# Four steps of a selective-scan layer moved one slot later in a hand-written schedule

## The chip, the cores and the metric

The kernel runs on one core of one Trainium2 chip. The metric is the device time of one execution in microseconds (us). All data are float32.

The engines have short names in the profile. PE is the matrix engine, and PEld is its weight load, which overlaps it. DVE is the vector engine, ACT the scalar engine, POOL the GpSimd engine, and SP the engine that issues most of the transfers. SBUF is the on-chip memory, and PSUM the small memory that PE writes its products to.

## The reference

The input x has the shape (2, 128, 64, 64): two images of 128 channels with 64 x 64 = 4096 positions. Four operators follow each other:

1. an embedding (a 128 x 128 product), two layers of a state-space model with a feed-forward net, an output product and a residual;
2. self-attention over the 4096 positions, whose query, key and value come from 3 x 3 convolutions;
3. self-attention whose query, key and value come from 1 x 1 products;
4. a multi-scale block: convolutions at four scales, a small attention over the scales, a layer norm and a fusion.

The change touches the two layers of operator 1 alone. One of these layers computes, for the tokens t of an image:

```
r = t;  x = layernorm(t)
u, z = split(x @ in_w.T);  u = silu(causal_conv4(u) + conv_b)
dt, B, C = split(u @ xproj_w.T);  dt = softplus(dt @ dt_w.T + dt_b)
h[n] = exp(dt * A[n]) * h[n] + dt * u * B[n]      # along the positions, 16 states n, 256 channels
y = sum_n h[n] * C[n] + u * ssm_D                 # the skip term
y = y * silu(z)                                   # the gate
t = y @ out_w.T + r                               # the mixer's output and its residual
t = t + ffn_w2 @ gelu(ffn_w1 @ layernorm(t))      # with biases
```

## The kernel before

**Items and slots.** The layers work on items. An item is a chunk of 512 positions of one image in one layer, so there are 2 images x 2 layers x 8 chunks = 32 items, in this order. For each item the scan is done in 32 steps of 128 rows x 512 positions: 8 groups (`g`, 32 channels each, four states side by side on the partitions make 128 rows) with 4 steps each. Each step is a *slot*. The outer loop (`for i in range(-2, NI + 2)`) runs over items, the inner one over the 32 slots. A period is one turn of the outer loop.

**What a slot always issues,** in this order: at the first slot of a group the transfers of dt for a later group (`spread_dt`), the product that spreads dt*u for the next group into the one PSUM buffer `pdu` (`spread_dtu`, L334, PE), and every second group the product that sums h over the states into `py` (`y_pair`, L373, PE, for two groups at once); then the scan of this slot (L358, DVE); the decay of four slots later (L347, ACT, four PSUM buffers `da`, so it waits for the scan of its own slot); after the last slot of a group, on POOL, a copy of the carries (L360) and the product of h with C (L361); and on DVE `times_b` (L340), which makes h for the next group from B and `pdu`. The h buffers are a ring of five that also holds `hid`, the feed-forward net's hidden values; a new h thus waits until the product `py` of an old one has been computed.

**The background steps.** All other work of the layers is spread over the slots by `background(i)`: `at(t, f, ...)` puts a step into slot t of period i. Steps go out behind the scan, the decay and `times_b` of their slot. Each engine takes its instructions in the order in which they are issued; no scheduler reorders them. In period i the scan belongs to item i, n = i + 1 is prepared (convolution and projections), p = i - 1 is finished (second half of y, gate, mixer, second layer norm), q = i - 2 ends its feed-forward net, and r = i + 2 is embedded and normalised. An item has an embedding (`embed`, L187; `embed_out`, L191) if r is in the first layer, and an output product (`out_mm`, L429; `out_add`, L434) if q is in the second.

**The steps that the change names.**
- `y_out` (L381, DVE): u = u * D + py, for one half (128 channels) of an item. It reads `py` in PSUM. Half 0 of item i is due in its own period, half 1 in the next.
- `gate` (L384, POOL): z = z * u over both halves.
- `mix_out` (L390 and L391, PE): the mixer's product into the PSUM buffer `po`, with the residual added through an identity.
- `mix_add` (L394, ACT): copies `po` back into the image.

**What is issued near them.** On DVE the scans and `times_b`. On PE, behind `py` in slot 4, the last convolution taps (L262), a z projection (L275), the feed-forward net's second product (L415 and L417), `pdu`, and then `mix_out`. On ACT a long row starts at `mix_add`: the silu with two table loads (L282 and L283, slot 11), `embed_out` or `out_add`, the squares and centred values of the layer norms (L203 and L204, from `pc`, L196), `dbl` (L295, from `pd`, L291), and the softplus with its table loads (L315 and L316, slot 17), with decays between them. The softplus frees `dtu` (L321, POOL, slot 18) and `var` (L210, PE); behind `var` come `ve` (L214, ACT) and further decays, behind `dtu` come h of that group and `nt` (L226, POOL), and then `nt` on ACT (L227, slot 20) and decays again. `ln_scale` (L239, DVE) waits for `pr` (L235, PE) in slot 28.

The loop that issues a slot:

```
if 0 <= t < NT:
    scan(t)
if 0 <= t + 4 < NT:
    decay(t + 4)
if m == 3 and 0 <= g + 1 < NG:
    times_b(g + 1)
for f, a in todo[t_]:
    f(*a)
```

Of the kernel before, what the change touches and what calls it, by code (L numbers as in the profile page):

```python
# [67 lines left out]
def tile_conv_seq(ctx: ExitStack, tc, x, consts, vecs, wemb, wlay, wconv, wdt, wqkv, wsmall, wms, out):  # L68
# [39 lines left out]
    with ExitStack() as s, tc.manual_schedule():  # L108
# [25 lines left out]
        for l in range(NL):  # L134
# [15 lines left out]
            for g in range(4):  # L150
                pa = mm.tile([P, NJ, DS], F32, name="pa", tag="mm")
                nc.tensor.matmul(pa.rearrange("p j n -> p (j n)"), lhsT=four(g), rhs=an, start=True, stop=True)
                for q in range(4):
                    at = slice(32 * q, 32 * q + 32)
# [15 lines left out]
        def has(i):  # L170
            return 0 <= i < NI
# [265 lines left out]
        def background(i):  # L437

            todo = [[] for _ in range(NSL)]

            def at(t, f, *a):
                todo[t].append((f, a))

            n, p, q, r = i + 1, i - 1, i - 2, i + 2
            if has(q):
                at(3, gelu, q)
                at(6, ffn_down, q, (0, 1)), at(7, ffn_down, q, (2, 3)), at(9, ffn_add, q)
                at(11, out_mm, q), at(12, out_add, q)
            if has(p):
                at(6, y_out, p, 1), at(6, gate, p)  # L450
                at(8, mix_out, p), at(10, mix_add, p)
            if has(n):
                at(0, pu_taps, n, 0, (0, 1)), at(1, pu_taps, n, 0, (2, 3)), at(2, pu_out, n, 0)
                at(3, pu_taps, n, 1, (0, 1)), at(4, pu_taps, n, 1, (2, 3)), at(5, pu_out, n, 1)
                at(13, xproj, n), at(14, xproj_out, n), at(14, spread_bc, n)
                at(15, dtproj, n, 0), at(16, dtproj, n, 1), at(17, soft_plus, n), at(18, dt_end, n)
            if has(i):
                at(1, pz_mm, i, 0), at(3, pz_out, i, 0)
                at(5, pz_mm, i, 1), at(6, pz_out, i, 1)
            if has(i) or has(n):  # L460
                at(11, silu, i, n)
            pair = [(k, second) for k, second in ((p, True), (r, False)) if has(k)]
            if has(r):
                at(10, embed, r), at(11, embed_out, r)
            w, m = {}, len(pair)
            for k, (it, second) in enumerate(pair):
                at(12 + 2 * k, ln_centre, w, k, it)
                at(13 + 2 * k, ln_square, w, k, it)
                at(27, ln_spread, w, k, m), at(28, ln_scale, w, k, it)
                at(29, ln_shift, w, k, it, second)  # L470
            if pair:
                at(17, ln_var, w, m), at(18, ln_eps, w, m), at(19, ln_rs, w, m), at(20, ln_newton, w, m), at(21, ln_step, w, m)
            if has(p):
                for f in range(4):
                    at(30 + f // 2, ffn_up, p, f)
            if has(i):
                at(23, y_out, i, 0)
            return todo

        eps = wp.tile([P, 1], F32, name="eps")  # L480
# [4 lines left out]
        for i in range(-2, NI + 2):  # L485
            todo = background(i)
            for t_ in range(NSL):
                t = i * NSL + t_
                g, m = divmod(t, 4)
                if m == 0 and 0 <= g + 3 < NG:  # L490
                    spread_dt(g + 3)
                if m == 0 and 0 <= g + 1 < NG:
                    spread_dtu(g + 1)
                if m == 0 and g % 2 == 1 and 0 <= g - 3 < NG:
                    y_pair(g - 3)
# [8 lines that stand above are left out]
# [667 lines left out]
```

## Time and profile before

| what | value |
|---|---|
| median of 3 runs | 5333.72 us (5329.3 to 5339.19) |
| span of the profiled execution | 5331.3 us |
| layers (0 to about 2190 us): PE, DVE, ACT, POOL busy | 1908, 1893, 1511, 1444 us |
| both attentions (to about 4490 us): PE, DVE busy | 2256, 1364 us |
| multi-scale block (to the end): PE, DVE busy | 745, 540 us |
| granted PE clock in these three stages | 0.88, 0.99, 0.94 |
| scans (L358) | 1024, 1265 ns each |
| `times_b` (L340) | 256, 2264 ns each |
| h times C (L361) | 256, 4532 ns each |
| skip terms (L381) | 64, 746 ns each |
| gate (L384) | 32, 2361 ns each |
| copy of `po` (L394) | 32, 588 ns each |

In a line of the timeline the first number is the start in us from the span's beginning and the second the time to the end of the group. Then follow the engine, the line of the kernel, the operation, what it writes and reads, and how many instructions were merged; in brackets stands how long the engine was idle before it and what ended that. PE's ends are modelled. A clock of 0.50 means that PE was granted half its full speed.

### The profile page before, as it was taken

Reading aid. Unit: us, or ns where it says so; the run is one execution under the profiler, and the core shown is the slowest. Engines: PE = TensorE matmul, PEld = TensorE weight load, DVE = VectorE, ACT = ScalarE, POOL = GpSimd, SP = SyncE. Lnnn points to the kernel's source line nnn. Section 1 sums busy time; section 2 is a strip of 40 time slices with the busy share of each in tenths; the row PEclk is TensorE's granted clock in tenths of the full one; section 3 lists DMA queues with packets and bytes.
Section 4 is the critical chain, followed back from the end, with each engine's and each line's share of the span. In section 5 each row is a group of like instructions: output and inputs, shape, how many; then the busy total and the mean of one; then the engine's idle time right before and its main releaser. Section 6 shows DMA issues by size and latency. Waiting matters only on the chain.

```text
span 5331.3 us, 48726 instructions
## 1 busy us (share of the span) xinstructions
PE 4908.7 (92%) x15085; PEld 2306.1 (43%) x15085; DVE 3796.5 (71%) x3810; ACT 2326.8 (44%) x2933; POOL 2286.9 (43%) x1948
## 2 busy tenths in 40 slices
PE   5899899999988997899999999999999998988997
PEld 1222222222222222356665566656666665333332
DVE  4999999999999999046663366657767775656665
ACT  4677777777777776212221122223223221223332
POOL 3766766666667667012221122223333332322221
PEclk8888988888888888999999999999999999999998
DMA  4222222222233332024442244444444442000000
GB/s 112 67 64 66 66 69 69 70 68 65 64 69 75 73 70 51 18 53 96 95 95 51 49 96 95 95 104 110 113 101 97 112 112 71 4 4 4 6 6 8
DMA packets 233843, 362.04 MB, mean 68 GB/s; under 512 B 87648, under 2 KB 88048, under 8 KB 225136
## 3 DMA queue, kind: packets, MB, share of 16 engines
q1 hardware_dynamic: 184432, 291.76, 23.3%
q10 hardware_dynamic: 49152, 67.17, 5.3%
q8 instruction: 121, 1.98, 0.2%
q14 instruction: 138, 1.13, 0.1%
HBM read 83.92 MB, written 6.29 MB: 17 GB/s over the span
## 4 chain that ended last, share of the span: by engine, by line
PE 58%; DVE 13%; POOL 12%; issue 7%; DMA 3%; ACT 3%; SPq 3%; ACTq 0%; DVEq 0%; POOLq 0%
PE pq L600 12%; PE po L647 12%; POOL h L361 9%; PE py L373 5%; PE pp L544 5%; DVE tr L627 4%; PE pu L262 3%; SPq L638 3%; PE pf L861 2%; DVE h L358 2%; DMA pt<-tr 2%; PE pdu L334 2%; PE ph L403 2%; PE pqkv L888 2%; PE pqq L544 2%
## 5 line engine op out<-in xcount | busy, mean ns | idle before, releaser
L634 POOL COPY pt<-tr 32x512 f32<-32x512 f32 x1024 | 628.0, 613 | 1680.6 <-DVE tr L627 912.0
L358 DVE TENSOR_TENSOR_SCAN h<-da,carry,h 128x512 f32<-128x512 f32 x1024 | 1241.1, 1265 | 52.0 <-ACT da L347 21.5
L361 POOL TENSOR_TENSOR h<-h,cb 128x2048 f32<-128x2048 f32 x256 | 1160.1, 4532 | 20.7 <-POOL carry L360 0.2
L604 DVE TENSOR_SCALAR_CACHE_REDUCE sc<-pq 128x1024 f32<-128x1024 f32 x512 | 625.6, 1222 | 761.0 <-PE pq L600 748.8
L647 PE MATMUL po<-pt,vt 128*128 128x256 f32 x4096 | 968.0, 380 | 4.1 <-DMA pt<-tr 4.1
L600 PE MATMUL pq<-k,q 128*128 128x512 f32 x2048 | 962.1, 592 | 4.8 <-ACT q L532 3.4
L647 PEld LDWEIGHTS po<-pt,vt 128*128 128x128 f32 x4096 | 776.4, 190 | 264.4 <-issue 174.6
L347 ACT ACTIVATE da<-dtb,am 128x512 f32<-128x512 f32 x1024 | 687.6, 685 | 273.0 <-DVE h L358 265.6
L613 ACT ACTIVATE sc<-sc,nm 128x4096 f32<-128x4096 f32 x128 | 474.8, 3710 | 723.2 <-DVE nm L611 628.0
L627 DVE STREAM_TRANSPOSE tr<-sc 128x2048 f32<-128x2048 f32 x256 | 589.2, 2302 | 37.7 <-DMA pt<-tr 24.2
L340 DVE TENSOR_TENSOR h<-bb,pdu 128x2048 f32<-128x2048 f32 x256 | 579.5, 2264 | 41.1 <-issue 28.5
L373 PE MATMUL py<-h,sel 128*32 128x512 f32 x2048 | 521.1, 654 | 0.5 <-POOL h L361 0.5
L600 PEld LDWEIGHTS pq<-k,q 128*128 128x128 f32 x2048 | 383.5, 190 | 277.8 <-issue 248.7
L334 PE MATMUL pdu<-dtu,fsel 128*128 128x512 f32 x512 | 334.4, 740 | 125.5 <-DVE h L340 123.0
L373 PEld LDWEIGHTS py<-h,sel 128*32 128x32 f32 x2048 | 117.6, 120 | 428.0 <-issue 422.4
L532 ACT ACTIVATE q<-pqq,vec 128x256 f32<-128x256 f32 x64 | 30.3, 473 | 606.4 <-PE pqq L544 361.2
L544 PE MATMUL pp<-xt,wq 128*128 128x512 f32 x576 | 250.2, 595 | 6.8 <-DMA wq<-in_wqkv 6.4
L262 PE MATMUL pu<-xn,wu 128*128 128x512 f32 x512 | 245.1, 612 | 3.3 <-ACT xn L252 1.7
L334 PEld LDWEIGHTS pdu<-dtu,fsel 128*128 128x128 f32 x512 | 97.1, 219 | 342.5 <-DVE h L340 219.6
L888 PE MATMUL pqkv<-f,ws 128*128 128x512 f32 x384 | 197.4, 640 | 10.2 <-ACT q L895 6.3
L950 DVE TENSOR_TENSOR ov<-v,pw 128x2048 f32<-128x2048 f32 x64 | 146.1, 2283 | 60.2 <-PE pw L943 60.0
L360 POOL COPY carry<-h 128x4 f32<-128x4 f32 x256 | 47.6, 186 | 317.4 <-DVE h L358 313.7
(191 smaller groups left out, 5138.1 us busy)
## 6 DMA issues: line engine op xcount, KB each, us to landing
pt<-tr SPq DMA_DIRECT2D x2048, 64.0 KB, 2.0
dtb<-dt SPq DMA_DIRECT2D x1024, 64.0 KB, 2.0
pt<-tr ACTq DMA_DIRECT2D x1024, 64.0 KB, 2.1
bb<-dr SPq DMA_DIRECT2D x128, 256.0 KB, 4.5
cb<-dr SPq DMA_DIRECT2D x128, 256.0 KB, 7.6
xt<-in_x SPq DMA_DIRECT2D x16, 256.0 KB, 5.1
xr<-in_x SPq DMA_DIRECT2D x16, 256.0 KB, 2.9
out<-ot SPq DMA_DIRECT2D x16, 256.0 KB, 2.0
```

The costliest lines, as they stand in the source:

```text
L334: nc.tensor.matmul(pdu, lhsT=four(s_ % 4), rhs=st[i]["dtu"][:, s_ // 4, :], start=True, stop=True)
L340: nc.vector.tensor_tensor(h, st[i]["bc", 0], pdu.unsqueeze(1).to_broadcast([P, 4, CH]), ALU.mult)
L347: nc.scalar.activation(da, st[i]["dtb", s_], AF.Exp, scale=am[items[i][1]][:, j, gg, m : m + 1])
L358: nc.vector.tensor_tensor_scan(h[:, m, :], da, h[:, m, :], carries[b, l][:, j, gg, m : m + 1], ALU.mult, ALU.add)
L361: nc.gpsimd.tensor_tensor(h, h, st[i]["bc", 1], ALU.mult)
L373: nc.tensor.matmul(py[r : r + 32, :], lhsT=sel, rhs=st[i]["h", s_ + k][:, m, :], start=(m == 0), stop=(m == 3), tile_position=(0, r),)
L544: nc.tensor.matmul(ps, lhsT=wq[:, which, tap, :], rhs=rhs, start=(tap == 0), stop=(tap == 8))
L600: nc.tensor.matmul(pq[:, i, :], lhsT=st["q", r, grp][:, it * P : (it + 1) * P], rhs=st["k"][:, at : at + CH], start=True, stop=True)
L604: nc.vector.tensor_scalar(dst, pq, 1.0, None, ALU.mult, ALU.max, accum_out=st["mx"][:, c2 : c2 + 1])
L627: nc.vector.transpose(tr, half.rearrange("p (t r f) -> p r t f", r=NB, f=32))
L634: nc.gpsimd.tensor_copy(dst, src)
L647: nc.tensor.matmul(st["po", r, grp], lhsT=st["vt"][:, jt, :], rhs=rhs, start=(jt == 0), stop=(jt == N // P - 1))
```

## The change

Five calls of `at` get a slot that is one later: both halves of the skip term, the gate, the mixer's product (slots 8 and 9 hold no other background product), and, from slot 10 to 11, the copy of its result. No instruction is added, removed or altered. In slot 11 the copy is still issued ahead of the silu.

```diff
             if has(p):
-                at(6, y_out, p, 1), at(6, gate, p)
-                at(8, mix_out, p), at(10, mix_add, p)
+                at(7, y_out, p, 1), at(7, gate, p)
+                at(9, mix_out, p), at(11, mix_add, p)
...
             if has(i):
-                at(23, y_out, i, 0)
+                at(24, y_out, i, 0)
```

## The prediction

> **What bounds the kernel now.** I read the engine shares and the slices of the page first, then the granted clock over one period of the layers, then the waits of line 381, then the timelines of the four engines over that period.
>
> ```profile
> PE 4908.7 (92%) x15085; PEld 2306.1 (43%) x15085; DVE 3796.5 (71%) x3810; ACT 2326.8 (44%) x2933; POOL 2286.9 (43%) x1948
> PEclk8888988888888888999999999999999999999998
> ```
>
> The edited lines run only in the first 16 to 17 slices (to about 2190 us). There PE is nearly always busy, at a granted clock of 0.88, and DVE is 86% busy (1892.88 of 2190 us). Neither share says which waits decide, so I follow one period (32 slots, one item). The 32 executions of the gate (line 384) start 64.80 to 64.90 us apart in 16 of the 31 intervals. This is one such period, cut where the clock changes; columns are busy time of PE, PEld, DVE, ACT, POOL, then clock:
>
> ```profile
> 370.56:377.38 6.82, 5.38 (x6) 0.85 (x6) 5.70 (x5) 5.70 (x8) 4.70 (x3) 0.50 1.05 229
> 377.38:384.21 6.83, 5.91 (x22) 1.79 (x22) 6.01 (x5) 5.01 (x9) 5.92 (x5) 1.00 0.72 156
> 384.21:394.45 10.24, 7.13 (x14) 1.41 (x15) 10.14 (x10) 4.49 (x7) 8.31 (x4) 0.50 0.23 57
> 394.45:435.40 40.95, 40.41 (x110) 13.47 (x106) 36.97 (x28) 31.47 (x45) 25.93 (x11) 1.00 0.10 26
> ```
>
> PE is solid for the last 41 us and runs twice at half clock. The stretches are 2, 2, 3 and 12 times 3.413 us, together 19.
>
> DVE (start, duration, what; in brackets its idle time before):
>
> ```profile
> 376.89 1.28 DVE L358 TENSOR_TENSOR_SCAN h<-da,carry,h 128x512 f32<-128x512 f32 x1 [1.02 <-ACT da L347]
> 378.09 2.26 DVE L340 TENSOR_TENSOR h<-bb,pdu 128x2048 f32<-128x2048 f32 x1
> 381.18 0.75 DVE L381 SCALAR_TENSOR_TENSOR u<-u,vec,py 128x512 f32<-128x512 f32 x1 [0.82 <-PE py L373]
> 381.84 4.80 DVE L358 TENSOR_TENSOR_SCAN h<-da,carry,h 128x512 f32<-128x512 f32 x4
> ...
> 411.62 0.75 DVE L381 SCALAR_TENSOR_TENSOR u<-u,vec,py 128x512 f32<-128x512 f32 x1 [2.16 <-PE py L373]
> ```
>
> The two skip terms make DVE wait for py, 0.82 us at slot 23 and 2.16 us at slot 6 (over the run 91.5 us in 57 waits). ACT and POOL in the same period:
>
> ```profile
> 354.67 0.68 ACT L347 ACTIVATE da<-dtb,am 128x512 f32<-128x512 f32 x1
> 357.40 0.59 ACT L394 COPY xt<-po 128x512 f32<-128x512 f32 x1 [2.06 <-PE po L391]
> 357.89 0.70 ACT L347 ACTIVATE da<-dtb,am 128x512 f32<-128x512 f32 x1
> 371.26 1.26 ACT L315 ACTIVATE dt<-pt,vec 128x512 f32<-128x512 f32 x2
> ...
> 372.60 2.34 POOL L321 TENSOR_TENSOR dtu<-dt,u 128x1024 f32<-128x1024 f32 x1 [4.85 <-ACT dt L315]
> 379.66 1.27 POOL L226 TENSOR_TENSOR nt<-nt,ve 2x512 f32<-2x512 f32 x1
> ...
> 388.88 2.08 PE L334 MATMUL pdu<-dtu,fsel 128*128 128x512 f32 x2 [3.11 <-DVE h L340]
> ```
>
> ACT waits 2.06 us for the mixer's po with a decay queued behind it, and then runs without a gap until after dt. So the loop is: PE solid from pdu (388.88) to the next po (422.21); the mixer's residual copy and 15.1 us of ACT to the end of dt; then either var on PE, ve, the last decay and scan 23 on DVE, or dtu, h and nt on POOL and decay 25 on ACT; then DVE's scans 25 to 27 and line 340, and pdu again.
>
> **What the Trainium skill says.** "TensorE: Matmul & The Clock Gate", Part 1 (What's actually happening): the clock is 4/8 or 8/8 and is judged over a free-running window of 4096 cycles at 1.2 GHz, 3413 ns. The trace agrees: only 0.50 and 1.00, changes 3.413 us apart, and a period of 19 x 3.413 = 64.85 us. The same page, Architectural detail: ACT, DVE and GpSimd queues are strict FIFO; the decay at 357.89 stuck behind the copy shows it. "GPSIMD Engine Reference", section 1: GpSimd shares its SBUF interface with VectorE where the latter has two SBUF inputs. Line 361's time here is 4503 to 4568 ns whatever DVE does, so I charge the moved gate nothing for new neighbours.
>
> **The change part by part.** Nothing is added or removed; no DMA is in the moved steps, and the order on SP and on PE stays as it was. Only DVE, ACT and POOL swap neighbours.
>
> 1. Second skip term, slot 6 to 7. DVE runs scan 7 (1.18 us, its decay was done at about 405.7) inside the 2.16 us wait. Line 340 then stands ahead of the skip term; it writes the h buffer that py reads (five buffers), so it waits for the same py and starts at about 411.65 instead of 413.48. DVE is about 1.2 us ahead at slot 8. Downstream PE is solid, and the next line 340 needs pdu at its end (about 0.3 us of the gain goes there); nothing on PE waits for DVE until pdu at slot 28. On the period: 0.
>
> 2. Gate, slot 6 to 7. It now stands behind h of that group on POOL: scan 7 ends at 410.7, carry and h to 415.5, gate to 417.9 (2.36 us). po starts at 419.50: slack 1.6 us, so 0.
>
> 3. Residual copy, slot 10 to 11 (mix_out, 8 to 9, has no PE neighbour to pass). The decay of slot 11 now runs in the 2.06 us wait ahead of the copy, so the silu and all behind it to dt come 0.62 us earlier. That holds where PE keeps ahead: in items with an embed alone pd and pc allow it; with out_mm alone pd allows 0.17; with both, PE's pc and pd bind and it is about 0. var, ve and scan 23 follow: 0.62 us.
>
> 4. First skip term, slot 23 to 24. Before: line 340 ends at 380.35, waits to 381.18, skip term, scan 24, and scan 25 starts at 383.04. After (0.62 earlier): 379.73, scan 24 to 381.0, py is ready, skip term to 381.75, scan 25. Decay 25 by the POOL path (dt, dtu, h, nt) is ready at 381.6, so it hardly binds. Gain at scan 25: 1.29 us, of which 0.67 from this step. Scans 26, 27 and line 340 carry it to pdu.
>
> Sum at the same half-clock loss: nine periods with embed alone x 1.3 = 11.7; eight with out_mm alone x 0.83 (0.17 + 0.66) = 6.6; two at the tail x 0.8 = 1.6; eight with neither x 0.7 (there 0.6 from ACT, and POOL's path limits step 4) = 5.6; four with both 0 (scan 25 there waits for decay 25 already, 0.19 us). Together 25.5 us.
>
> The clock. PE restarts at 388.88 and stays at half clock to 394.45: (394.45 - 388.88) / 2 = 2.79 us lost. The window it restarts in began at 387.63, 1.25 us earlier. If PE starts before that edge, a full window makes it warm at 391.04: an early item does so (restart at 195.50, py takes 4.79 us instead of 5.38). Short of the edge a gain is eaten: restarting earlier by d costs d/2 more, so the period stays at 19 windows until the loss reaches that of a restart at the edge, (394.45 - 387.63) / 2 = 3.41, that is for gains up to 3.41 - 2.79 = 0.62 us. Both 0.83 and 1.3 pass it. Then the restart drifts over the window, the loss lies between 1.71 and 3.41, on average 2.56, 0.23 less: 17 periods x 0.23 = 4 us more. If the out_mm periods, which pass narrowly, stay locked, it is 18 + 2 = 20 us. I take 28.
>
> The sum is against the profiled span of 5331.3 us, inside the other runs (5329.3 to 5339.2); from the median 5333.7 it gives 5306.
>
> **Rivals.** (A) Locked: the half-clock window swallows the gain and most periods stay at 64.85. For: neighbouring periods agree to 0.03 us, and items with both embed and out_mm, with 0.9 to 1.7 us more on PE, have nearly the same (64.73 to 65.12). Against: the early periods and those with neither (63.13, 63.79) do run free. Time: only the neither periods gain, 5334 - 6 = 5328. (B) Larger gain: the free periods settle on 18.5 windows (63.15, as one period does now) or the first half-clock stretch shortens as well: 27 x 1.7 = 46 us, 5288. (C) Slower: the gate now behind h is late for po. It has 1.6 us at 419.50; were scan 7 not ready to run before py, gate would end at 412.8 + 7.2 = 420.0, PE would idle 0.5 us in every item and everything behind it too, DVE's gain would be void, and 32 x 0.5 = 16 us gives 5350. It decides once gate comes over 1.6 us later than worked out. Against: decay 7 precedes the gelu on ACT and is done 5 us before. (D) Hidden: POOL's path to decay 25 binds more than I think, leaving step 3 alone: 9 x 0.62 + 8 x 0.17 + 8 x 0.6 = 11.8 us, 5322.
>
> **How the numbers follow.** Forecast 0.55, (A) 0.13, (B) 0.14, (C) 0.08, (D) 0.10. A difference of 0.2%, 10.7 us, is about what a measurement tells from none. Faster takes the forecast, (B) and (D): 0.79; same is (A): 0.13; slower is (C): 0.08. The range reaches from (B) to just past (A): 5284 to 5332. The forecast's own range is 5296 to 5318.
>
> **What would show it.** After: the waits of line 381 fall from 91.5 us to under 20; the copy at line 394 no longer has a decay between it and the silu's table load; gates come unevenly, about 63 to 64 us apart, instead of 64.85; PE's restart stretches are half-clock for 2 or 3 windows in turn; behind 2190 us all stages keep their length. Wrong if gates stay 64.85 apart with line 381's wait gone (A), or if po waits for z (C).

## The result, and the profile after

The changed kernel takes 5298.99 us (median of 4 runs, 5296.11 to 5301.44) against 5333.02 for the one before (4 runs too): the ratio is 0.9935, with a 95% interval of 0.9918 to 0.9952. It is 34 us faster; the forecast was 28 us. The two executions that were profiled differ by 37.3 us (spans of 5331.3 and 5294.0).

The engine shares and the clock row of the page after:

```profile
PE 4882.0 (92%) x15085; PEld 2303.4 (44%) x15085; DVE 3801.3 (72%) x3810; ACT 2328.5 (44%) x2933; POOL 2288.2 (43%) x1948
PEclk8899889888989898899999999999999999999998
```

The instructions are as many as before, and DVE, ACT and POOL are as busy. PE's busy time is 27 us less, with more 9s in the clock row of the layers (6 against 1 in its first 17 slices): the same products ran for less time at half clock.

The waits of DVE at line 381 (us in total, times); before it was 91.5 us in 57 waits:

```profile
  PE py L373: 8.6, 1
```

The timeline of DVE, and behind the dots those of ACT, POOL and PE, in the period that answers to the one shown of before:

```profile
376.59 1.28 DVE L358 TENSOR_TENSOR_SCAN h<-da,carry,h 128x512 f32<-128x512 f32 x1
377.79 0.72 DVE L381 SCALAR_TENSOR_TENSOR u<-u,vec,py 128x512 f32<-128x512 f32 x1
379.57 3.63 DVE L358 TENSOR_TENSOR_SCAN h<-da,carry,h 128x512 f32<-128x512 f32 x3 [1.06 <-ACT da L347]
...
408.38 2.29 DVE L340 TENSOR_TENSOR h<-bb,pdu 128x2048 f32<-128x2048 f32 x1 [1.01 <-PE py L373]
410.58 0.74 DVE L381 SCALAR_TENSOR_TENSOR u<-u,vec,py 128x512 f32<-128x512 f32 x1
...
378.24 0.72 ACT L227 ACTIVATE nt<-nt,c 2x512 f32<-2x512 f32 x1 [2.80 <-POOL nt L226]
378.87 3.88 ACT L347 ACTIVATE da<-dtb,am 128x512 f32<-128x512 f32 x6
...
416.15 1.29 ACT L347 ACTIVATE da<-dtb,am 128x512 f32<-128x512 f32 x2
419.00 0.59 ACT L394 COPY xt<-po 128x512 f32<-128x512 f32 x1 [1.56 <-PE po L391]
419.60 1.28 ACT L282 ACT_TABLE_LOAD   x1
432.26 1.27 ACT L315 ACTIVATE dt<-pt,vec 128x512 f32<-128x512 f32 x2
...
412.19 2.37 POOL L384 TENSOR_TENSOR z<-z,u 128x1024 f32<-128x1024 f32 x1
...
416.22 1.88 PE L390 MATMUL po<-z,wl 128*128 128x512 f32 x4
```

The first skip term (377.79) stands behind a scan and no longer waits. Line 340 (408.38) waits for py in place of the second one. On ACT two decays (416.15) run ahead of the copy of po, and the silu's table load follows the copy at once. The gate ends at 414.56 and po starts at 416.22, so it had 1.66 us to spare. That holds for most periods, but not for the first one, where PE waits for the gate:

```profile
160.67 3.78 PE L390 MATMUL po<-z,wl 128*128 128x512 f32 x4 [3.77 <-POOL z L384]
```

New in the period shown is the 1.06 us that scan 25 (379.57) waits for its decay, which stands behind the nt step of ACT, which waits for POOL.

The last gate starts at 2109.6 us, 35.1 us earlier than before (2144.7). What follows it takes 3184.4 us, against 3184.5 in a kernel in which only the second skip term and the gate are moved (below). So all of the gain lies in the layers.

The table gives the mean distance between two gates in us, by what the period holds, with the number of such periods in brackets. The last two periods are left out. Where the gate was moved, the first period, with an embedding, holds PE's wait for it. The distances are those of one profiled run each, which can lie some us from the median: that of the delay took 5345.7 us and was the slowest of its 13.

| kernel | us (median) | embed alone (9) | neither (8) | out_mm alone (8) | both (4) |
|---|---|---|---|---|---|
| before | 5333.0 | 64.71 | 63.99 | 64.86 | 64.88 |
| changed | 5299.0 | 63.20 | 62.44 | 63.72 | 64.86 |
| mixer's output and copy alone | 5319.1 | 63.34 | 63.10 | 64.77 | 64.91 |
| first skip term alone | 5312.8 | 63.92 | 63.17 | 63.50 | 64.61 |
| second skip term and gate alone | 5333.5 | 64.97 | 63.99 | 64.86 | 64.88 |
| before, with a delay on ACT | 5341.3 | 64.63 | 64.88 | 64.82 | 65.03 |
| changed, second skip term and gate put back | 5305.7 | 63.29 | 62.87 | 63.72 | 64.96 |
| changed, newton step later | 5280.4 | 62.49 | 62.35 | 63.16 | 63.99 |
| before, PE kept busy | 5279.6 | 62.32 | 62.38 | 62.37 | 63.87 |
| changed, PE kept busy | 5254.9 | 61.42 | 61.84 | 61.95 | 63.77 |
| changed, both | 5239.1 | 61.31 | 61.07 | 61.44 | 62.40 |

### The profile page after: what moved, and what is told of

It reads as the page before. It is cut to its first block, busy times and chain, and to the rows that moved or that the text cites. A ratio compares the mean times of both kernels' runs of the same rounds, so it can differ in the third digit from the quotient of the medians.

```text
span 5294.0 us, 48723 instructions
## 1 busy us (share of the span) xinstructions
PE 4882.0 (92%) x15085; PEld 2303.4 (44%) x15085; DVE 3801.3 (72%) x3810; ACT 2328.5 (44%) x2933; POOL 2288.2 (43%) x1948
## 4 chain that ended last, share of the span: by engine, by line
PE 47%; POOL 22%; issue 11%; DVE 10%; SPq 4%; DMA 3%; ACT 3%; ACTq 0%; DVEq 0%; POOLq 0%
POOL h L361 17%; PE pq L600 12%; PE po L647 12%; PE pp L544 5%; DVE tr L627 4%; SPq L638 3%; DMA pt<-tr 2%; PE pf L861 2%; PE pqkv L888 2%; PE pqq L544 2%; PE py L373 1%; PE pw L943 1%; POOL dtu L321 1%; POOL z L384 1%; PE pfus L1008 1%
```

## The experiments

My theory had two parts. Two moves (the copy behind a decay on ACT, and the first skip term) shorten the loop. And the loop is held at whole clock windows of 3.413 us by the half clock at which PE restarts, so that small gains and small delays are swallowed. The rivals were that gains simply add up, and that the second skip term's wait of 2.16 us was what held the loop. A period of 64.8 to 64.9 us is called held here, a shorter one free.

**One part alone.** The mixer's output and the copy:

```diff
-                at(8, mix_out, p), at(10, mix_add, p)
+                at(9, mix_out, p), at(11, mix_add, p)
```

> Only mix_out and mix_add are moved (slots 9 and 11); skip terms and gate stay. Theory (window lock): in the periods with an embedding ACT's row to dt starts 0.62 us earlier, but the period is held at 19 windows (64.85 us) for gains up to 0.62, so about nothing comes of it there; the eight periods with neither embed nor out_mm run free and gain 0.6 each: about 5328. Rival (gains simply add up): 9 x 0.62 + 8 x 0.17 + 8 x 0.6 = 12 us, 5321. Rival (the two skip terms are all that matters): 5333.

Measured: 5319.05 us, ratio 0.9967 (0.9954 to 0.9979). The periods with out_mm stay at 64.77 as expected. Those with an embedding get free, which I had put just out of reach of 0.62 us. They then gain 1.37 us, over twice what the move takes from ACT's row. Gates of three of these periods:

```profile
220.72 2.35 POOL L384 TENSOR_TENSOR z<-z,u 128x1024 f32<-128x1024 f32 x1 [4.03 <-DVE u L381]
283.28 2.36 POOL L384 TENSOR_TENSOR z<-z,u 128x1024 f32<-128x1024 f32 x1 [4.02 <-DVE u L381]
346.95 2.36 POOL L384 TENSOR_TENSOR z<-z,u 128x1024 f32<-128x1024 f32 x1 [4.02 <-DVE u L381]
```

They lie 62.56 and 63.67 us apart, together 126.23; 37 windows of 3.4133 us are 126.29. The loop has gone from 19 windows to 18.5 on average. So neither the strict lock nor the plain sum was right in size, though the total, 5319, lies near the plain sum (5321).

The periods with out_mm alone, for which 0.17 us was worked out, show the restart taking back part of a small gain. In one of them PE restarts at 1985.65 us, 4.50 us after the clock fell, and gets its full clock back at 1991.39; in the kernel before, the same restart (2003.38) comes 4.67 us after the fall, and the full clock at 2008.96. So the restart comes earlier against the clock, spends 5.74 in place of 5.58 us at half clock, and loses half of that, 2.87 in place of 2.79 us. The periods themselves are 64.85 us in both.

The first skip term:

```diff
-                at(23, y_out, i, 0)
+                at(24, y_out, i, 0)
```

> Only the first skip term is moved (slot 23 to 24). Without the earlier ACT row its gain ends where decay 25 is ready (382.2 in the shown period of before, scan 25 started at 383.04): at most 0.7 us. Window lock: 0.7 is just at the edge of what 64.85 us holds, so the periods either stay or get free by little: 5323 to 5333. Rival (gains add up): 17 x 0.67 = 11 us, 5322. The wait of line 381 at slot 23 goes; the 2.16 us at slot 6 stay.

Measured: 5312.77 us, ratio 0.9955 (0.9943 to 0.9968), and 72.2 us in 32 waits left at line 381. All but the periods with both get free. It gains more than either theory gave. Each against its own kernel before, the two parts gain 15.7 and 21.9 us, some 38 together, about as much as the whole change (34), but not in the same kinds of period.

The second skip term and the gate:

```diff
-                at(6, y_out, p, 1), at(6, gate, p)
+                at(7, y_out, p, 1), at(7, gate, p)
```

> Only the second skip term and the gate are moved (slot 6 to 7). Theory: line 340 takes over the wait for py, DVE gains 1.2 us at slot 8, PE is solid behind it and nothing comes of it: 5333, within 3 us. Rival (the 2.16 us wait was what held the loop): 27 periods x 1.2 = 32 us, 5301, that is the whole gain of the change.

Measured: 5333.5 us, ratio 0.9999 (0.9991 to 1.0007). The longer of the two waits was worth nothing by itself, and the periods with neither or with out_mm alone are unchanged to 0.01 us: the rival falls. Two effects at the ends cancel. From scan 27 of the first item to that of the third it takes 3.6 us longer (PE waits 3.77 us for the first gate, as in the changed kernel). From scan 27 of the last item but one to the end it takes 3.4 us less (3264.8 against 3268.2).

**A delay of known size.** A copy whose result nobody reads, behind the silu:

```diff
             nc.scalar.preload_act_table_set(EXP_LN_SET)
+            nc.scalar.copy(spare, kc)
```

> The kernel before with one added ACT copy of 128x656 behind the silu in slot 11 (about 0.7 us by the 128x512 and 128x1024 rows), whose result is not used: a delay of known size in ACT's row to dt. Theory (window lock): the half-clock loss at PE's restart can fall from 2.79 to 1.71 us, so the periods held at 64.85 us stay there to within 0.05 us and only the eight free periods and the ends pay: 5340. Rival (no lock): every period is 0.7 us longer, 65.5 us, and the time is 30 x 0.7 = 21 us longer, 5354.

Measured: 5341.28 us, ratio 1.0011 (1.0003 to 1.0019). The delay itself, in the timeline of ACT:

```profile
365.62 0.74 ACT L284 COPY spare<-kc 128x656 f32<-128x656 f32 x1
```

It holds ACT's row up by 0.64 us (the next instruction starts at 366.26) in every period. The held periods did not get longer (64.63 and 64.82 against 64.71 and 64.86), and the free ones went from 63.99 to 64.88: they were caught too. Three gates of periods with neither:

```profile
609.55 2.36 POOL L385 TENSOR_TENSOR z<-z,u 128x1024 f32<-128x1024 f32 x1 [2.85 <-DVE u L382]
674.25 2.36 POOL L385 TENSOR_TENSOR z<-z,u 128x1024 f32<-128x1024 f32 x1 [4.01 <-DVE u L382]
739.07 2.36 POOL L385 TENSOR_TENSOR z<-z,u 128x1024 f32<-128x1024 f32 x1 [4.02 <-DVE u L382]
```

The distances are 64.70 and 64.82 us. About 6.6 us were paid where some 20 us of delay were put in. The time is the one that the theory gave (5340), but the delay was not swallowed where the theory had it. PE's restart loses 2.77 us in the period shown, against 2.79. What gave way is the other product at half clock, var. First the kernel before, then the one with the delay, in the same period (the line numbers behind the added one are higher by 1):

```profile
372.00 3.57 PE L210 MATMUL var<-sq,kc 128*2 128x512 f32 x4 [1.54 <-ACT dt L315]
375.61 0.68 ACT L214 ACTIVATE ve<-var,eps 2x512 f32<-2x512 f32 x1 [1.08 <-PE var L210]
```

```profile
375.05 2.39 PE L210 MATMUL var<-sq,kc 128*2 128x512 f32 x4 [1.54 <-ACT dt L316]
377.51 0.66 ACT L214 ACTIVATE ve<-var,eps 2x512 f32<-2x512 f32 x1
```

With the delay the clock fell at 376.27, in the middle of var; before, it had fallen at 370.56, ahead of it. From the start of dt to that of ve it is 4.35 us before (371.26 to 375.61) and 3.20 with the delay (374.31 to 377.51). That is 1.15 us less, more than the 0.64 us put in. All eight periods with out_mm alone go the same way: var took 3.57 us in each before, and takes 1.88 in six and 2.33 in two with the delay. In the free periods var takes 3.57 us with the delay, and these paid. So there are two places where the half clock takes time and can give it back, and my theory knew one. The table adds them up over 30 periods. The restart's loss is half of the time from the start of pdu in slot 28 to the return of the full clock. Var's stretch goes from the start of var to that of ve: 2.47 us at full clock, 3.61 at half.

| kernel | loss at the restart, us | var's stretch, us |
|---|---|---|
| before | 79.3 | 100.7 |
| before, with a delay on ACT | 79.4 | 88.6 |
| mixer's output and copy alone | 77.3 | 92.7 |
| first skip term alone | 70.7 | 93.5 |
| changed | 70.1 | 91.6 |

With either move alone both sums are smaller than before, so a gain beyond the moves' own can come from there. How much of var's stretch reached the period was not measured: POOL's path to decay 25 can end later than var's.

**The second skip term with the others.** The changed kernel with that part undone:

```diff
-                at(7, y_out, p, 1), at(7, gate, p)
+                at(6, y_out, p, 1), at(6, gate, p)
```

> The changed kernel with the second skip term and the gate put back to slot 6; first skip term and the mixer's residual copy stay moved. Theory: these two moves carry the whole gain, so 5299, within 4 us, although line 381 waits for py again at slot 6 (some 2 us in most periods). Rival (DVE's earlier start at slot 8 matters once the periods run free): 5305 to 5315.

Measured: 5305.67 us, ratio 0.9947 (0.9934 to 0.9959), as the rival had it. The part that is worth nothing alone is worth 6.7 us beside the others, by the two medians; the two intervals overlap, but no single run of one kernel reaches those of the other (5304.28 and more, 5301.44 and less). About half of it shows in the periods with neither (62.87 against 62.44, eight times 0.43 = 3.4 us). There PE does not run solid: it catches up with DVE at the pdu of slot 12. First the kernel with the part undone, then the changed one:

```profile
610.60 1.13 PE L334 MATMUL pdu<-dtu,fsel 128*128 128x512 f32 x2 [0.66 <-DVE h L340]
```

```profile
606.40 1.09 PE L334 MATMUL pdu<-dtu,fsel 128*128 128x512 f32 x2
```

Another 3.0 us lie between scan 27 of the last item but one and the end (3268.2 against 3265.2), as in the run in which this part was moved alone.

**The wait that the change uncovered.** The decay of scan 25 put ahead of the nt step:

```diff
-at(20, ln_newton, w, m), at(21, ln_step, w, m)
+at(21, ln_newton, w, m), at(22, ln_step, w, m)
```

> The changed kernel with ln_newton and ln_step one slot later too (21 and 22), so that on ACT decay 25 stands ahead of the nt step that waits for POOL. Theory (the POOL path by dtu, h and nt to decay 25 is now what ends the loop): scan 25 no longer waits for its decay (1.06 us in the shown period after the change), 0.5 to 1 us in the periods with an embedding or with neither: 5280 to 5288. Rival (PE's own row binds): 5299.

Measured: 5280.35 us, ratio 0.9901 (0.9888 to 0.9915), within the theory's figures. ACT's timeline now has two decays ahead of the nt step, done before its wait:

```profile
377.10 1.28 ACT L347 ACTIVATE da<-dtb,am 128x512 f32<-128x512 f32 x2
379.41 0.72 ACT L227 ACTIVATE nt<-nt,c 2x512 f32<-2x512 f32 x1 [1.03 <-POOL nt L226]
```

In the second image four periods with an embedding follow each other at 61.37, 61.41, 61.42 and 61.43 us: 18 windows are 61.44. PE's restart settles against the clock meanwhile: it comes 3.31, 3.25, 3.21 and 3.19 us after the clock fell. This is the clearest sign of the lock.

**The half clock taken away.** Products on PE that nobody reads, two in slot 25 and three in slot 27, into the PSUM buffer that is free there:

```diff
+        def keep_busy(i, n):
+            o = yp.tile([P, CH], F32, name="idle", tag="y")
+            for _ in range(n):
+                nc.tensor.matmul(o, lhsT=four(0), rhs=st[i]["dtu"][:, 0, :], start=True, stop=True)
...
+                at(25, keep_busy, i, 2), at(27, keep_busy, i, 3)
```

> The changed kernel with added products on PE whose results are not used: two in slot 25 and three in slot 27, about 0.86 us each, in PE's idle time around pr; everything else is computed as before. Theory (PE restarts in slot 28 at half clock because it idled, and loses 1.7 to 3.4 us in each period): it restarts at full clock, the solid stretch is about 2.5 us shorter, and the loop gains what the other engines let through, 1 to 2.5 us in 28 periods: 5230 to 5271. Rival (the half clock costs nothing because DVE, ACT or POOL bind at the same place): 5299, or later by what the added products delay pr and pdu, up to 15 us.

Measured: 5254.85 us, ratio 0.9852 (0.9838 to 0.9865). The stretches between changes of the clock (columns as in the prediction), and PE's restart:

```profile
361.40:368.20 6.80, 5.28 (x7) 0.84 (x6) 5.61 (x5) 5.68 (x8) 4.39 (x3) 0.50 0.81 174
368.20:484.20 116.00, 111.31 (x305) 36.11 (x304) 111.89 (x85) 87.52 (x125) 85.48 (x40) 1.00 0.29 66
...
377.39 2.84 PE L440 MATMUL idle<-dtu,fsel 128*128 128x512 f32 x6
380.07 1.02 PE L334 MATMUL pdu<-dtu,fsel 128*128 128x512 f32 x2
381.02 3.63 PE L373 MATMUL py<-h,sel 128*32 128x512 f32 x16
```

pdu takes 1.02 us and py 3.63, where they took 2.08 and 5.38 at half clock; PE runs 116 us at full clock, through two restarts. More work on PE made the kernel 44 us faster. Four consecutive periods with an embedding are equal at 61.52 to 61.54 us, and not a multiple of the window: PE's restart moves on against the clock by 0.09 us in each of them (11.35, 11.44, 11.53 and 11.61 us after the clock rose) and does not settle. Var still runs at half clock in most periods; only the restart was freed.

Both together:

> The changed kernel with both: ln_newton and ln_step in slots 21 and 22, and the five unused products on PE per period. Theory: the gains of the two add up, 5215 to 5255. Rival (one of them already removes what the other does): no better than the better of the two.

Measured: 5239.10 us, ratio 0.9824 (0.9811 to 0.9837), the fastest version: it beats the changed kernel by 60 us. The two gains (18.6 and 44.1 us, 62.7 in sum) nearly add up, as the theory had it.

The kernel before, with the same unused products:

> The kernel before (all five calls at their old slots) with the same five unused products per period on PE. Theory (window lock): without the half clock at PE's restart nothing holds the period at 64.85 us any more; periods of one kind are equal among themselves but differ between kinds, the periods with an embedding fall to 64.85 - 2.79 = 62.1 us or a little above, and the five moved calls are then worth the plain sum of their steps, about 25 to 30 us: 5280 to 5285 against the 5255 of the changed kernel with the same products. Rival (the half clock has nothing to do with the 64.85): the periods stay at or above 64.85, 5334 or later. Rival (the moves are worth what they were, 35 us, in any clock): 5290.

Measured: 5279.63 us, ratio 0.9903 (0.9887 to 0.992). The periods with an embedding alone fall to 62.32 us, about the 62.1 of the theory, so the half clock at the restart did hold them. But they are not equal among themselves, as the theory had them: behind the first one they run from 62.08 to 62.70. Nor do the kinds differ much, but for the one with both. Against 5254.85 us, the five moved calls are worth 24.8 us where PE restarts at full clock. Single runs of the two kernels lie 19.4 to 27.4 us apart, and the two profiled ones are at the lower end.

## Why the prediction was right

- **The total and the direction.** 5299 lies in the range and in the forecast's own range (5296 to 5318); the gain is a fifth larger than forecast. The signs named came too: line 381 waits 8.6 us, PE's restart stretches are half-clock for two or three windows in turn, and nothing changes behind the layers.
- **Step 1, second skip term: 0.** Right alone (0.9999), and line 340 took over the wait as worked out. Wrong beside the others: "nothing on PE waits for DVE until pdu at slot 28" was read from a period with an embedding, and does not hold where PE has less to do. This term of the sum was some 6.7 us instead of 0.
- **Step 2, gate: 0.** Right in the period that it was read from: the slack was put at 1.6 us and is 1.66. In four other periods it is 0.6 to 0.7. Rival (C), a gate late for po, came in the first period alone, where PE waited 3.77 us (160.67). There the gate had only 2.0 us to spare before, against 4.7 in the period that the prediction took for all.
- **Step 3, copy behind the decay: 0.62 us.** Right in size: from the copy to dt it is 13.86 us before (357.40 to 371.26) and 13.26 after (419.00 to 432.26). Right too that it gives little with out_mm alone (64.77) and nothing with both. Alone it gave 1.37 us with an embedding; the excess over 0.62 goes with shorter stretches at half clock, at the restart and at var (the table behind the delay's run).
- **Step 4, first skip term: 0.67 us.** The wait of line 381 is gone. But POOL's path "hardly binds" holds only while var runs at half clock. In the period shown after the change var runs at full clock, and ve, and with it scan 23, no longer wait for it:

```profile
369.28 1.88 PE L210 MATMUL var<-sq,kc 128*2 128x512 f32 x4 [1.54 <-ACT dt L315]
371.75 0.66 ACT L214 ACTIVATE ve<-var,eps 2x512 f32<-2x512 f32 x1
```

So DVE is ahead of POOL's path, and scan 25 waited 1.06 us for it. Putting that decay ahead of the nt step was worth 18.6 us.
- **The sum without the clock: 25.5 us.** With the half clock at the restart taken away, the change is worth 24.8 us by the medians, 19.5 by the profiled runs. The division by kinds of period did not come out: there the periods gain 0.90 us with embed alone, 0.42 with out_mm alone and 0.54 with neither, where 1.3, 0.83 and 0.7 were worked out. The periods with both gain 0.1, as good as nothing, as forecast. So the nearness of 25.5 to 24.8 is in part luck.
- **The clock term: 4 us.** This is the term that was mis-sized. By the medians 34 - 24.8 leaves about 9 us for it, by the profiled runs 37.3 - 19.5 leaves 18. The loss at the restart fell by 9.2 us (79.3 to 70.1 in the same table), over twice the 4 us forecast. I let the restart drift evenly over a window. Instead the freed loop tends to patterns of whole windows over two or three periods: two of the changed kernel's periods with an embedding sum to 62.60 + 63.72 = 126.32 us (37 windows: 126.29), and three with out_mm to 63.87 + 64.38 + 62.91 = 191.16 (56 windows: 191.15). The same three in the second image, 63.96 + 62.69 + 63.77 = 190.42, don't. Rival (B) named the 18.5 windows; the periods with an embedding did go near there. The prediction put nothing on var, whose stretch is 9.1 us shorter in sum; what that was worth stays open. Rival (A), all held, did not come, but its mechanism shows in the periods with out_mm alone when only the copy is moved.

## What to carry to other kernels

A wait in the engine that looks busiest is worth what stands behind it: the longer of DVE's two waits gave nothing alone, while one decay that a copy had kept from running on ACT gave 16 us, part of it by way of the clock. In a loop in which one engine falls to half clock at each turn, ask first whether the period is a multiple of the clock's window. If so, small gains and delays may not show, or may show larger than they are, until a few of them together move the loop to another multiple. A right total does not say which stretch at half clock swallowed them: look at each in the trace. Filling the idle time with products that nobody reads was the largest single gain here, and it makes the worth of other changes easier to read. And read the first period too, not only one in the middle.

## What the runs showed of the hardware

- The window of PE's clock can set the period of a whole loop of five engines: 64.85 us (19 windows) in one kernel, with PE's restart 4.65 to 4.67 us after the clock's fall in all eight periods with out_mm alone, and 61.37 to 61.43 us (18 windows) in another. With the restart at full clock, equal periods were 61.52 to 61.54 us and no multiple.
- The four var products took 3.57 us at half clock and 1.88 at full clock. When 0.64 us of work was added on ACT in each period, the shorter time at var gave it back; the loss at the restart did not change (79.3 and 79.4 us in 30 periods).
- Five added products per period (4.8 us of PE's time in the period shown) kept PE at full clock through its restart; pdu and py took 2.8 us less together, and the kernel gained 44 us.
